# Graph network on one core: the first layer's block chain cut into two pieces, four sets of gathered rows, sums held by pairs of blocks

## The chip, the cores and the metric

The kernel runs on one core of a Trainium2 chip. A core has a matrix engine (TensorE, PE in the profile; its weight loads are listed as PEld), a vector engine (VectorE, DVE), a scalar engine (ScalarE, ACT), a general engine that here issues the gathers (GpSimd, POOL) and a queue engine that only starts transfers (SyncE, SP). Each engine works through its own list of instructions in order; semaphores tie the lists together. The tables and inputs lie in device memory (HBM), the tiles in on-chip memory (SBUF), and the results of matmuls in PSUM, which has eight banks.

The metric is the device time of one execution in microseconds, lower is better. The kernel before took 4373.74 us (median of six runs, 4352.41 to 4384.59).

## The reference, cut to what matters

Four graph layers follow each other on 6250 nodes with 128 features and about 106250 edges, sorted by their target node. Each layer is followed by a residual sum and a layer norm. The change lies in the first layer, a graph attention layer with four heads of 32 features:

```
xp = (x @ W).reshape(n, HEADS, OUT_C)
a_src = jnp.einsum('nhc,hc->nh', xp, att_src)
a_dst = jnp.einsum('nhc,hc->nh', xp, att_dst)
e = a_src[src] + a_dst[dst]                      # src, dst: the edges and one more loop per node
e = jnp.where(e >= 0, e, NEG_SLOPE * e)
m = jax.ops.segment_max(e, dst, num_segments=n)
ex = jnp.exp(e - m[dst])
denom = jax.ops.segment_sum(ex, dst, num_segments=n)
out = jax.ops.segment_sum((ex / denom[dst])[:, :, None] * xp[src], dst, num_segments=n)
return jax.nn.relu(out.reshape(n, HEADS * OUT_C) + bias)
x = _layernorm(x + the layer above)
```

So every edge fetches the row of its source node, the largest logit of each target node is found, each row is weighed with an exponential, and the rows of each target node are added up. Layers two to four (an edge-gated sum, a linear attention with a graph convolution, and a sum with two batch norms) are not touched.

## The kernel before

**Blocks.** The 6250 nodes are 50 blocks (`NB`) of 125 (`BN`). The edges of one block's targets are laid on 128 partitions (`P`) with 18 edges (`CE`) each. `quick_layer0` runs one loop over the 50 blocks (line 823); all of it is unrolled.

**One block, in the order of the source.**

1. Gather: a tile `rows` of 128 x 18 x 138 numbers, from three buffers. ACT writes its last two columns (lines 825 and 826), and POOL issues 18 indirect DMAs (line 828), each of which fetches one row of 136 numbers for each of the 128 partitions. A buffer can be filled anew only when the matmuls of the block three before have read it.
2. `dr` (lines 833 and 834, two buffers): SP loads the targets of the block's edges, the same for all of 125 partitions; DVE compares them with the partition's number (line 844); 18 small matmuls (line 848) bring each edge the terms of its target into `own_ps`, one PSUM bank.
3. `m` (line 851, two buffers): DVE compares the edges' targets with the numbers 0 to 124, which lie in PSUM as `node_ps` (a bank of its own). The result, 128 x 18 x 125, tells the summing matmuls which edge goes to which node.
4. The largest logit: ACT copies the targets and the gathered source terms (`az`) into `side`, a tile in one PSUM bank with one buffer (lines 856 and 861). DVE marks which edges of a partition have different targets (`off`, lines 857 and 859), adds (`each`, 864) and takes the maximum (`top`, 867). Twelve matmul passes (line 870, `sh_ps`) bring the maxima of neighbouring partitions, because one node's edges can reach over several.
5. The weights: DVE reduces `own_ps` to `own` (873), combines the neighbours' maxima (`near`, `carry`, `far`, `top`, 875 to 883), forms `z` (885 to 889); ACT takes the exponential into `side` (`ex`, 891) and copies it into `rows` (892); DVE multiplies the rows with it (896, "the weighing").
6. The sums: 18 matmuls in full precision (36 records in the trace; helper `gathered`, line 341) add up the rows of each node into a PSUM tile with two buffers. They wait for the weighing and are what frees the `rows` buffer and the `m` buffer.

**Work that is put off.** The functions in `left_over` are run one block later: `to_acc` copies the sums into `acc`, a tile for all 50 blocks (ACT, line 819), and after each second block `finish` (line 783) closes a pair: it adds the loop edge, divides, adds the bias and x, normalises (`norm_few`) and, through `table1`, turns the two blocks with matmuls (`t_ps`, lines 924 to 928) and stores the rows of the second layer's table. For the first 18 pairs `count` (line 1091) counts edges for later layers with 18 matmuls a pair (line 1099) and some DVE and ACT work; `sort_keys` does the groundwork in two portions (blocks 0 and 8).

**What sets the order.** No order is written out here, except on SP (`issue_after`). The framework's planner simulates the program and issues, on each engine, whatever it finds ready, earlier source first. So an instruction can stand many places ahead of its place in the source; in the trace `m` of a block is computed one block early. On the chip each engine keeps to the order planned. The framework also derives all waits: for data, for buffers to come free, and for two engines that touch one PSUM bank.

After the loop, lines 915 and 916 copy two columns of `acc` (`indeg`, `selfs`) for the second layer, whose gathers need the complete table.

Of the kernel before, what the change touches and what calls it, by code (L numbers as in the profile page):

```python
# [8 lines left out]
F32 = mybir.dt.float32  # L9
I32 = mybir.dt.int32  # L10
AF = mybir.ActivationFunctionType
ALU = mybir.AluOpType
# [11 lines left out]
N, F, BN, NB = 6250, 128, 125, 50  # L24
P, CE, NCHUNK = 128, 18, 6144
CPP = NCHUNK // P
NONE = NCHUNK - P
HEADS, OC, SLOPE = 4, 32, 0.2
# [9 lines left out]
FEW = 2  # L38
# [8 lines left out]
BF16 = mybir.dt.bfloat16  # L47
# [4 lines left out]
def kernel(ctx: ExitStack, tc: tile.TileContext, a: dict, out: bass.AP):  # L52
    nc = tc.nc
# [19 lines left out]
    indeg = const.tile([BN, NB], F32, name="indeg")  # L73
# [66 lines left out]
    def flat(t):  # L140
        return t.rearrange("p b f -> p (b f)")
# [585 lines left out]
    def quick_layer0(table):  # L727
        with tc.tile_pool(name="q0", bufs=1) as st, tc.tile_pool(name="q0w", bufs=2) as wk:
# [17 lines left out]
            acc = st.tile([BN, NB, W0], F32, name="acc")  # L746
# [36 lines left out]
            def finish(b0):  # L783
# [3 lines left out]
                nc.vector.tensor_tensor(own[:, 1], acc[:, sl, M0:M0 + HEADS], xp[:, sl, M0:M0 + HEADS], op=ALU.add)  # L787
# [12 lines left out]
                nc.vector.tensor_tensor(r, r, acc[:, sl, :F], op=ALU.add)  # L800
                rden = wk.tile([BN, FEW, HEADS], F32, name="rden")
                nc.vector.tensor_tensor(rden, acc[:, sl, A0:A0 + HEADS], part, op=ALU.add)
# [6 lines left out]
                nc.vector.scalar_tensor_tensor(flat(r), flat(r), 0.0, flat(X[:, sl, :]), op0=ALU.max, op1=ALU.add)  # L809
                norm_few(wk, b0, r, FEW)  # L810
                table1(ps, wk, w1, b0, r)

            with tc.tile_pool(name="q0_ps", bufs=2, space=PSUM) as ps:
                node_ps = ps.tile([P, BN], F32, name="node_ps", bufs=1)
                nc.scalar.copy(node_ps, node)
                left_over = []

                def to_acc(b, s):
                    nc.scalar.copy(acc[:, b, :], s)
                    if b % FEW == FEW - 1:  # L820
                        finish(b - FEW + 1)

                for b in range(NB):
                    rows = wk.tile([P, CE, W0], F32, name="rows", bufs=3)
# [6 lines left out]
                    d = dl[:, b, :]  # L831

                    dr = wk.tile([BN, P * CE], BF16, name="dr")
# [8 lines left out]
                    if b % 2 and b // 2 + 1 < NB // BPE:  # L842
                        split_terms(b // 2 + 1)
                    nc.vector.tensor_scalar(dr, dr, lane[:BN], None, op0=ALU.is_equal)
                    dr_g = dr.rearrange("d (p g) -> d g p", g=CE)
                    own_ps = ps.tile([P, CE, 6 * HEADS], F32, name="own_ps", bufs=1)
                    for g in range(CE):
                        nc.tensor.matmul(own_ps[:, g, :], dr_g[:, g, :], pieces[:, b].rearrange("p q s -> p (q s)"),  # L848
                                         start=True, stop=True)
                    m = wk.tile([P, CE, BN], F32, name="m")  # L850
                    nc.vector.tensor_tensor(m, node_ps[:, None, :].to_broadcast([P, CE, BN]),  # L851
                                            d[:, :, None].to_broadcast([P, CE, BN]), op=ALU.is_equal)

                    off = wk.tile([P, CE, CE], F32, name="off", bufs=1)
                    side = ps.tile([P, 1 + 2 * HEADS, CE], F32, name="side", bufs=1)
# [13 lines left out]
                    for k in range(2 * SPAN):  # L869
                        nc.tensor.matmul(sh_ps[:, k, :], shift[:, k, :], top[:, :, CE - 1] if k < SPAN else top[:, :, 0],  # L870
                                         start=True, stop=True)
                    own = wk.tile([P, 2 * HEADS, CE], F32, name="own")
# [19 lines left out]
                    nc.scalar.copy(rows[:, :, A0:A0 + HEADS], ex)  # L892
# [4 lines left out]
                    s = gathered(ps, m, rows, W0)  # L897
# [8 lines left out]
                    left_over.append(lambda b=b, s=s: to_acc(b, s))  # L906
# [4 lines left out]
                    if b % 2 and b // 2 < EARLY:  # L911
                        left_over.append(count(ps, wk, nth, b // 2))
                for later in left_over:
                    later()
            nc.vector.tensor_copy(indeg, acc[:, :, W0 - 2])
            nc.vector.tensor_copy(selfs, acc[:, :, W0 - 1])
# [785 lines left out]
```

## Time and profile before

| What | Value |
| --- | --- |
| Time, median of six runs | 4373.74 us (4352.41 to 4384.59) |
| The profiled execution | 4340.48 us, span 4338.7 us |
| First layer's gathers, first start to last end | 85.0 to 1411.1 us |
| First gather of the second layer | 1459.55 us |
| Busy in the span | PE 56%, DVE 50%, ACT 22%, POOL 54% |
| First layer's 900 gathers | 871.2 us busy, 968 ns each, 455.8 us of idle time before them |
| Granted TensorE clock, mean of the span | 0.707 |

The profile is one execution, recorded by the hardware. A group's line names the source line, the engine, the operation, what is written and read, how often, then the busy time and the mean duration, then the idle time of the engine just before such instructions and what ended most of it. "issue" is idle time in which the engine waited for nothing that the profile shows, "remote" means that a semaphore ended the wait and the profile does not find whose instruction set it. In a timeline a line has the start, the length, the engine, the source line, the operation, the tiles, the number of instructions merged and, in brackets, the engine's idle time before with its releaser. The starts of matmuls are recorded, their ends are modelled.

### The profile page before, as it was taken

Reading aid. Unit: us, or ns where it says so; the run is one execution under the profiler, and the core shown is the slowest. Engines: PE = TensorE matmul, PEld = TensorE weight load, DVE = VectorE, ACT = ScalarE, POOL = GpSimd, SP = SyncE. Lnnn points to the kernel's source line nnn. Section 1 sums busy time; section 2 is a strip of 40 time slices with the busy share of each in tenths; the row PEclk is TensorE's granted clock in tenths of the full one; section 3 lists DMA queues with packets and bytes.
Section 4 is the critical chain, followed back from the end, with each engine's and each line's share of the span. In section 5 each row is a group of like instructions: output and inputs, shape, how many; then the busy total and the mean of one; then the engine's idle time right before and its main releaser. Section 6 shows DMA issues by size and latency. Waiting matters only on the chain.

```text
span 4338.7 us, 46396 instructions
## 1 busy us (share of the span) xinstructions
PE 2422.0 (56%) x16000; PEld 1951.5 (45%) x16000; DVE 2179.0 (50%) x6589; ACT 948.9 (22%) x2088; POOL 2345.8 (54%) x2342
## 2 busy tenths in 40 slices
PE   2256644444444345454444444444758868978887
PEld 2245544433344234343444434344647657834444
DVE  2355555555554534454444445445747658733234
ACT  1011111111111101111111111111425435632224
POOL 4566666666666455655565555554653333066660
PEclk6566666666666566666666666666879879988888
DMA  3443233333332233333333333332323323255441
GB/s 106 93 99 74 71 74 78 79 81 75 78 76 65 73 99 94 103 97 94 94 100 91 98 97 98 93 95 75 101 84 107 106 85 116 108 194 168 158 155 56
DMA packets 187555, 422.00 MB, mean 97 GB/s; under 512 B 52792, under 2 KB 98868, under 8 KB 187300
## 3 DMA queue, kind: packets, MB, share of 16 engines
q0 software_dynamic: 88960, 214.29, 20.2%
q1 hardware_dynamic: 82026, 171.37, 11.3%
q10 hardware_dynamic: 16314, 33.19, 2.1%
q8 instruction: 129, 2.11, 0.2%
q14 instruction: 126, 1.03, 0.1%
HBM read 341.45 MB, written 77.23 MB: 96 GB/s over the span
## 4 chain that ended last, share of the span: by engine, by line
PE 30%; issue 18%; DVE 11%; another core or an unknown queue 4%; ACT 2%; POOL 1%; DMA 0%; DVEq 0%; ACTq 0%; POOLq 0%
PE acc_ps L1517 7%; PE theta L1025 7%; PE gathered L341 6%; PE acc_ps L1290 3%; DVE mw L1042 3%; DVE hit_d L1273 1%; DVE load L1220 1%; PE c_ps L1279 1%; POOL rows L1012 1%; PE s_ps L1478 1%; PE own_ps L972 1%; DVE hit_s L1270 1%; DVE to L1215 1%; DVE m L1562 1%
## 5 line engine op out<-in xcount | busy, mean ns | idle before, releaser
L1012 POOL DMA_INDIRECT rows<-table1q,e_all x900 | 879.2, 977 | 671.8 <-PE gathered L341 450.4
L828 POOL DMA_INDIRECT rows<-table0q,e_all x900 | 871.2, 968 | 455.8 <-issue 260.0
L1025 PE MATMUL theta<-parts,dr 125*128 125x128 bf16 x2700 | 355.2, 275 | 551.8 <-issue 541.5
L1025 PEld LDWEIGHTS <-dr 125*128 125x128 bf16 x2700 | 277.6, 154 | 630.4 <-issue 624.2
L1554 POOL DMA_INDIRECT rows<-table2q,e_all x252 | 291.8, 1158 | 364.0 <-PE pre_ps L1380 205.8
L341 PE MATMUL gathered<-rows,m 128*125 128x138 f32 x1800 | 342.7, 362 | 251.2 <-issue 129.9
L341 PEld LDWEIGHTS gathered<-rows,m 128*125 128x125 f32 x1800 | 321.5, 260 | 265.6 <-issue 138.8
L1554 POOL DMA_INDIRECT rows<-table3q,e_all x252 | 277.0, 1099 | 290.8 <-ACT x L1120 151.8
L1290 PE MATMUL acc_ps<-cs,x 125*128 125x250 bf16 x2700 | 397.9, 281 | 16.4 <-issue 16.0
L341 PE MATMUL gathered<-rows,mw 128*125 128x129 f32 x1800 | 302.8, 346 | 152.2 <-DVE mw L1042 138.8
L341 PEld LDWEIGHTS gathered<-rows,mw 128*125 128x125 f32 x1800 | 295.3, 258 | 157.2 <-DVE mw L1042 141.3
L1517 PE MATMUL acc_ps<-cs,x 125*128 125x500 bf16 x1350 | 325.6, 394 | 67.2 <-issue 50.9
L1290 PEld LDWEIGHTS <-x 125*128 125x128 bf16 x2700 | 272.6, 101 | 63.9 <-issue 20.9
L1280 ACT CAST cs<-c_ps 128x500 bf16<-128x500 f32 x450 | 255.4, 577 | 209.8 <-PE c_ps L1279 129.9
L851 DVE TENSOR_TENSOR m<-node_ps,dl 128x2250 f32<-128x2250 f32 x50 | 125.0, 2501 | 292.9 <-remote 260.1
L1042 DVE TENSOR_SCALAR mw<-node,dl,gw 128x125 f32<-128x125 f32 x900 | 245.7, 353 | 32.6 <-issue 28.7
L1517 PEld LDWEIGHTS <-x 125*128 125x128 bf16 x1350 | 133.0, 100 | 251.4 <-issue 116.9
L1279 PE MATMUL c_ps<-hit_d,hit_s 128*128 128x250 bf16 x900 | 186.5, 287 | 93.0 <-issue 63.0
L1029 DVE SCALAR_TENSOR_TENSOR junk<-theta,W 128x128 f32<-128x128 f32 x900 | 209.0, 284 | 15.1 <-remote 5.3
L1003 DVE TENSOR_TENSOR gram<-gram,gram_ps 128x129 f32<-128x129 f32 x25 | 7.3, 291 | 376.3 <-PE gram_ps L1002 376.3
L848 PE MATMUL own_ps<-pieces,dr 125*128 125x24 bf16 x900 | 63.1, 214 | 234.5 <-DVE own L873 143.7
L1026 DVE TENSOR_TENSOR theta<-theta,rows 128x512 f32<-128x512 f32 (+1 forms) x250 | 152.7, 638 | 62.7 <-remote 44.6
(364 smaller groups left out, 3940.0 us busy)
## 6 DMA issues: line engine op xcount, KB each, us to landing
dr<-dl_rows SPq DMA_DIRECT2D x100, 562.5 KB
counts<-cs SPq DMA_DIRECT2D x90, 625.0 KB
cs<-counts SPq DMA_DIRECT2D x45, 625.0 KB
cs<-counts ACTq DMA_DIRECT2D x45, 625.0 KB
rows<-table0q,e_all POOLq DMA_INDIRECT x900
rows<-table1q,e_all POOLq DMA_INDIRECT x900
rows<-table2q,e_all POOLq DMA_INDIRECT x252
rows<-table3q,e_all POOLq DMA_INDIRECT x252
```

The lines of the kernel that those rows point to most:

```text
L341: nc.tensor.matmul(s, m[:, g, :], rows[:, g, :], start=(g == last_first[0]), stop=(g == last_first[-1]))
L828: nc.gpsimd.indirect_dma_start(out=rows[:, g, :TW], out_offset=None, in_=table, in_offset=bass.IndirectOffsetOnAxis(ap=e_all[:, b, g:g + 1 ...
L1012: nc.gpsimd.indirect_dma_start(out=rows[:, g, :2 * F], out_offset=None, in_=table1_q, in_offset=bass.IndirectOffsetOnAxis(ap=e_all[:, b, g ...
L1025: nc.tensor.matmul(t[:, j, :], dr_g[:, g0 + j, :], y[:, k, :], start=(k == 0), stop=(k == 2))
L1026: follow(nc.vector.tensor_tensor(t[:, :n, :], t[:, :n, :], rows[:, g0:g0 + n, :F], op=ALU.subtract), b - 1)
L1029: nc.vector.scalar_tensor_tensor(junk, t[:, j, :], 0.0, w2, op0=ALU.max, op1=ALU.mult, accum_out=dot[:, g0 + j:g0 + j + 1])
L1042: last = nc.vector.tensor_scalar(mw[:, g, :], node, dl[:, b, g:g + 1], gw[:, g:g + 1], op0=ALU.is_equal, op1=ALU.mult)
L1279: nc.tensor.matmul(c_ps[:, i, :], hit_s[:, j, :, i], hit_d[:, j, :, i], start=True, stop=True)
L1280: nc.scalar.copy(cs[:, 2 * j:2 * j + 2, :], c_ps)
L1290: nc.tensor.matmul(acc_of[q], x3[:, k * SC + j, i, :], cs[:BN, j, :], start=(k == 0 and j == 0 and i == 0), stop=(k == NB // SC - 1 and j ...
L1517: nc.tensor.matmul(acc[:, :n, :], x3[:, k * SC + j, i, :], cs[:BN, :n, j, :], start=(k == 0 and j == 0 and i == 0), stop=False)
L1554: nc.gpsimd.indirect_dma_start(out=rows[:, g, :], out_offset=None, in_=table, in_offset=bass.IndirectOffsetOnAxis(ap=late_e[:, i, g:g + 1] ...
```

## The change

The loop body is cut into three functions. `gather(b)` gives out the rows buffer, the 18 gathers and the load of `dr`. `highest(b)` does the compare of `dr`, the matmuls into `own_ps`, `off`, `az`, `each`, `top` and the matmuls of the neighbours (`sh_ps`). `weigh(b)` makes `m`, reduces `own_ps`, finishes the maximum, takes the exponential, weighs the rows and adds them up. A round of the loop now reads: gather of block b, `weigh` of block b-1 with the put-off work (`step`), `highest` of block b.

What is held changes with it: `rows` has four buffers instead of three, `dr` three instead of two, `off` two instead of one, `own_ps` two banks instead of one. To pay for that bank, `node_ps` and two copies of `side` now share a single bank, in a tile named `bank`; blocks take the two copies in turn. `acc` for 50 blocks is gone; each pair has its own `acc` tile of two blocks (three buffers), and `finish` copies the pair's two columns to `indeg` and `selfs`, which replaces the two copies behind the loop. The copy of a block's sums into `acc` is ordered on ACT behind the copy of the next block's exponentials (`weighed`); this orders the list and adds no wait.

The diff, with the repeated index changes in `finish` left out:

```
-            acc = st.tile([BN, NB, W0], F32, name="acc")
...
-            def finish(b0):
+            def finish(b0, acc):
...
+                nc.vector.tensor_copy(indeg[:, sl], acc[:, :, W0 - 2])
+                nc.vector.tensor_copy(selfs[:, sl], acc[:, :, W0 - 1])
                 norm_few(wk, b0, r, FEW)
                 table1(ps, wk, w1, b0, r)
...
-                node_ps = ps.tile([P, BN], F32, name="node_ps", bufs=1)
+
+                n_side = (1 + 2 * HEADS) * CE
+                bank = ps.tile([P, 4 * P], F32, name="bank", bufs=1)
+                node_ps = bank[:, :BN]
+                side_of = [bank[:, BN + k * n_side:BN + (k + 1) * n_side].rearrange("p (h g) -> p h g", g=CE) for k in range(2)]
                 nc.scalar.copy(node_ps, node)
                 left_over = []
-
-                def to_acc(b, s):
-                    nc.scalar.copy(acc[:, b, :], s)
+                acc_of, weighed = {}, {}
+
+                def to_acc(b, s, after):
+                    if b % FEW == 0:
+                        acc_of[b // FEW] = wk.tile([BN, FEW, W0], F32, name="acc", bufs=3)
+                    copied = nc.scalar.copy(acc_of[b // FEW][:, b % FEW, :], s)
+                    if after in weighed:
+                        tc.add_manual_dep(copied.ins, weighed[after].ins.name, mybir.DependencyInfo(
+                            mybir.DependencyClass.NoSync, mybir.DependencyReason.DATA), reason="order")
                     if b % FEW == FEW - 1:
-                        finish(b - FEW + 1)
-
-                for b in range(NB):
-                    rows = wk.tile([P, CE, W0], F32, name="rows", bufs=3)
+                        finish(b - FEW + 1, acc_of.pop(b // FEW))
+
+                def gather(b):
+
+                    rows = wk.tile([P, CE, W0], F32, name="rows", bufs=4)
...
-                    d = dl[:, b, :]
-
-                    dr = wk.tile([BN, P * CE], BF16, name="dr")
+                    dr = wk.tile([BN, P * CE], BF16, name="dr", bufs=3)
...
+                    return rows, dr
+
+                def highest(b, rows, dr):
+
                     nc.vector.tensor_scalar(dr, dr, lane[:BN], None, op0=ALU.is_equal)
                     dr_g = dr.rearrange("d (p g) -> d g p", g=CE)
-                    own_ps = ps.tile([P, CE, 6 * HEADS], F32, name="own_ps", bufs=1)
+                    own_ps = ps.tile([P, CE, 6 * HEADS], F32, name="own_ps")
...
-                    m = wk.tile([P, CE, BN], F32, name="m")
-                    nc.vector.tensor_tensor(m, node_ps[:, None, :].to_broadcast([P, CE, BN]),
-                                            d[:, :, None].to_broadcast([P, CE, BN]), op=ALU.is_equal)
-
-                    off = wk.tile([P, CE, CE], F32, name="off", bufs=1)
-                    side = ps.tile([P, 1 + 2 * HEADS, CE], F32, name="side", bufs=1)
+                    d = dl[:, b, :]
+                    off = wk.tile([P, CE, CE], F32, name="off")
+                    side = side_of[b % 2]
...
+                    return b, rows, own_ps, off, top, sh_ps
+
+                def weigh(b, rows, own_ps, off, top, sh_ps):
+
+                    d = dl[:, b, :]
+                    side = side_of[b % 2]
+                    az = side[:, 1:1 + HEADS, :]
+                    m = wk.tile([P, CE, BN], F32, name="m")
+                    nc.vector.tensor_tensor(m, node_ps[:, None, :].to_broadcast([P, CE, BN]),
+                                            d[:, :, None].to_broadcast([P, CE, BN]), op=ALU.is_equal)
                     own = wk.tile([P, 2 * HEADS, CE], F32, name="own")
...
-                    nc.scalar.copy(rows[:, :, A0:A0 + HEADS], ex)
+                    weighed[b] = nc.scalar.copy(rows[:, :, A0:A0 + HEADS], ex)
...
-                    s = gathered(ps, m, rows, W0)
+                    return gathered(ps, m, rows, W0)
+
+                def step(b, s):
+
+                    nonlocal left_over
                     for later in left_over:
                         later()
...
-                    left_over.append(lambda b=b, s=s: to_acc(b, s))
+                    left_over.append(lambda: to_acc(b, s, b + 1))
...
+                behind = None
+                for b in range(NB):
+                    rows, dr = gather(b)
+                    if behind is not None:
+                        step(b - 1, weigh(*behind))
+                    behind = highest(b, rows, dr)
+                step(NB - 1, weigh(*behind))
                 for later in left_over:
                     later()
-            nc.vector.tensor_copy(indeg, acc[:, :, W0 - 2])
-            nc.vector.tensor_copy(selfs, acc[:, :, W0 - 1])
```

More of the change, by code (lines that the diff above doesn't have):

```diff
@@ L786, in finish @@
                 nc.vector.tensor_tensor(own[:, 0], xp[:, sl, A0:A0 + HEADS], xp[:, sl, M0:M0 + HEADS], op=ALU.add)
-                nc.vector.tensor_tensor(own[:, 1], acc[:, sl, M0:M0 + HEADS], xp[:, sl, M0:M0 + HEADS], op=ALU.add)
+                nc.vector.tensor_tensor(own[:, 1], acc[:, :, M0:M0 + HEADS], xp[:, sl, M0:M0 + HEADS], op=ALU.add)
                 own_f = own.rearrange("p k b h -> p (k b h)")
@@ L799, in finish @@
                                             part[:, j, :, None].to_broadcast(shape[:1] + shape[2:]), op=ALU.mult)
-                nc.vector.tensor_tensor(r, r, acc[:, sl, :F], op=ALU.add)
+                nc.vector.tensor_tensor(r, r, acc[:, :, :F], op=ALU.add)
                 rden = wk.tile([BN, FEW, HEADS], F32, name="rden")
-                nc.vector.tensor_tensor(rden, acc[:, sl, A0:A0 + HEADS], part, op=ALU.add)
+                nc.vector.tensor_tensor(rden, acc[:, :, A0:A0 + HEADS], part, op=ALU.add)
                 nc.vector.reciprocal(rden, rden)
```

## The prediction

> **What bounds the first layer now.** The gather line of the page, and that line's own view for what ended its idle time:
>
> ```profile
> span 4338.7 us, 46396 instructions
> ...
> L828 POOL DMA_INDIRECT rows<-table0q,e_all x900 | 871.2, 968 | 455.8 <-issue 260.0
> ```
>
> ```profile
> L828 POOL DMA_INDIRECT rows<-table0q,e_all x900: 941/947/1802, 85.0 to 1410.1; - x180
> ...
>   issue: 260.0, 850
>   remote: 99.9, 32
>   PE gathered L341: 90.4, 13
> ```
>
> POOL works from 85.0 to 1411.1 us. Between two gathers of one block lie 0.30 us that belong to the issue itself (850 times, 260 us); eighteen gathers cost 22.5 us. The other 195.8 us stand before a block's first gather, for a buffer. So the layer's ceiling for any better overlap is about 196 us, 4.5%. From block 19 on the blocks come every 25.6 us: 22.5 and a pause of about 3. Whom the pause waits for is seen in the timeline of two blocks:
>
> ```profile
> 1005.00 0.94 POOL L828 DMA_INDIRECT rows<-table0q,e_all  x1 [2.99 <-remote]
> ...
> 1030.26 0.28 ACT L819 COPY acc<-gathered 125x138 f32<-125x138 f32 x1 [10.06 <-remote]
> 1030.26 2.50 DVE L851 TENSOR_TENSOR m<-node_ps,dl 128x2250 f32<-128x2250 f32 x1 [6.00 <-remote]
> ...
> 1030.49 0.94 POOL L828 DMA_INDIRECT rows<-table0q,e_all  x1 [2.99 <-remote]
> ...
> 1032.75 0.16 DVE L875 TENSOR_TENSOR near<-sh_ps,gap 128x24 f32<-128x24 f32 x1
> ...
> 1037.52 1.28 ACT L891 ACT_TABLE_LOAD   x1
> 1038.81 0.29 ACT L891 ACTIVATE side<-z 128x72 f32<-128x72 f32 x1
> ...
> 1039.39 2.56 DVE L896 TENSOR_TENSOR rows<-rows,side 128x2304 f32<-128x2304 f32 x1 [3.31 <-ACT side L891]
> ...
> 1042.01 6.26 PE L341 MATMUL gathered<-rows,m 128*125 128x138 f32 x36 [4.80 <-issue]
> 1042.72 0.29 ACT L861 COPY side<-rows 128x72 f32<-128x72 f32 x1 [0.56 <-DVE off L857]
> ...
> 1055.98 2.50 DVE L851 TENSOR_TENSOR m<-node_ps,dl 128x2250 f32<-128x2250 f32 x1 [9.76 <-remote]
> ```
>
> ACT's copy of the sums, `m` and the next gather start together: three readers of one event, the end of the summing matmuls of three blocks' buffers ago. The block is one ring: weighing (to 1041.95), sums on PE (released at 1055.96), neighbours' matmuls behind them, `near` to `z` (3.4 us), exponential, weighing (2.56). From weighing to weighing that is 27.3 us (1014.7 to 1041.95) and 23.95 us (to 1065.9) in turn. Yet the releases stay 25.5 to 25.7 us apart, each about 3 us after POOL's eighteenth gather, whichever half it is. The matmuls too look quicker than they are: their 36 records begin and end within 6.3 us, the reader starts 14 us after the first. From block 18 on it is so in every block, until no gathers are left; then the reader follows at once:
>
> ```profile
> 1437.86 6.30 PE L341 MATMUL gathered<-rows,m 128*125 128x138 f32 x36 [1.09 <-DVE rows L896]
> 1444.19 0.27 ACT L819 COPY acc<-gathered 125x138 f32<-125x138 f32 x1 [7.12 <-PE gathered L341]
> ```
>
> So while POOL gathers, PE's results come 8 to 9 us late, and I can't name the resource. This weakens every saving on the ring.
>
> **The change part by part.**
>
> *The two stages.* They could overlap a block's `highest` with the `weigh` of the block before only if ACT may write the next `az` before DVE has read this block's `ex`. The trace says no: ACT's `az` copy (line 861) writes other columns of `side` than `off` (857) reads, and still starts 0.03 us after it, at 1042.72 after 1042.69; in the view of that line `off` releases it 22 times. Both copies of `side` and `node_ps` now lie in one bank, and in the source `weigh` of b-1 precedes `highest` of b. So `az` of b still follows the weighing of b-1, and I book nothing for the stages as such. If the two copies were free of each other, the 14 us of sums would cover near, exponential and weighing, and POOL's 22.5 us would be the bound: that is the lower end.
>
> The Trainium skill, "PSUM — Partial Sum Buffer", section "PSUM bank collisions raise a hardware error", has the same as a rule of the chip: two engines must not touch one bank in the same partitions together, other addresses and two readers included. By the rule the second `side` is worth nothing; by the row alone (a write behind a read) it is the same sum, and the rule only adds that `m`, a reader of that bank, must now keep clear of ACT as well.
>
> *`m` (2.50 us).* It stands in DVE's list before `near` and starts with the release, so it delays `near`: 2.3 us in one half (1056.1, when the neighbours' matmuls are through, to 1058.4), 1.05 us in the other (1031.7 to 1032.75). In the new source it needs `az` of its own block, so it comes after `top` and runs while PE still sums. Mean offer 1.7 us a block.
>
> *The pair's finish.* In every second block ACT stands before the exponential with the copies of `t_ps` and a table load: `z` is ready at 1036.1, the exponential starts at 1038.81, 2.7 us. The copy into `acc` now comes behind the next block's exponentials, so this work starts one exponential later, beside the sums; its four matmuls still wait behind them. Offer 1.35 us a block, half of it sure. What it moves: about 4.4 us of finish on DVE (lines 786 to 809 and 363 to 368, 18 instructions of 0.15 to 0.42 us) comes ahead of the next `off` (0.5 and 0.33), `each` (1.5), `top` (1.5) and `m` (2.5), with the compare of `dr` (0.84) 7.2 us. Together 11 to 12 us of DVE under 14 us of sums: hidden, but with 2 to 3 us to spare. If the sums took 7 us, as at 1437.86, 4 to 5 us would stick out.
>
> *The second `own_ps`.* DVE's reduce (line 873) waits in front of the chain, 57.2 us in 7 waits that its view calls remote (it waits for the matmuls into `own_ps` alone), most of it in the first blocks: 11.46 us at 199.75, 5.71 us at 441.92. Matmuls a block earlier into a second bank take the smaller ones. Between 0 and -57 I take -20; the longest, 16.52 us at 131.54, has POOL behind it and stays.
>
> *The fourth set.* POOL may fill one block more. In a ring that sets the pace this makes nothing quicker; POOL runs ahead once. At the end three instead of two blocks run without gathers, 14.4 to 15.8 us each (1414.0, 1429.8, 1444.2) instead of 25.6: -10. At the beginning the 21.1 us of POOL's first pause (153.2 to 174.3) fill up, but block 0's sums decide, not the gathers: 0. No transfer is added: 900 gathers, 50 loads of `dr` on SP, only earlier.
>
> *The small copies.* 50 copies in `finish` for 2 behind the loop, 0.2 us each on DVE, 10 us in all; DVE has half of its time idle and they end no chain. Without that cover, 10 us.
>
> **The sum.** `m` and finish offer up to 3.05 us a block, as much as POOL's pause (3.1). Over 49 blocks that would be -150. Against it stands that the release kept to POOL's run, not to the 27.3 or 23.95 us of its half. The ends are 0 and -150; I take a quarter, -38, because the row nearest to the question (equal releases from unequal halves) argues for little. With -20 and -10 that is -68: 4340.5 to 4272 for the profiled execution. It lies 33 us under the median of the runs, so I forecast 4305 us.
>
> **The rivals.**
>
> *POOL becomes the bound* (chance 0.13). The pauses vanish nearly all: 150 of the 195.8 us, 4224 us. For it: the ring's own work without delays is below 22.5 us. Against it: the shared bank and the late PE.
>
> *The wait comes back* (0.27). PE's results come with POOL's pause whatever the ring does; only the tail and a little of the start remain, -10 to -20: about 4360 us. For it: the equal releases. Against it: blocks 1 and 9, whose sums were read after 6.2 and 7.9 us.
>
> *Slower: four sets feed POOL without a pause, and PE is late as long as it gathers* (0.28). The place is the beginning, where three sets are filled back to back:
>
> ```profile
> 110.08 1.29 PE L848 MATMUL own_ps<-pieces,dr 125*128 125x24 bf16 x18 [17.74 <-issue]
> 131.54 0.61 DVE L873 TENSOR_REDUCE own<-own_ps 128x144 f32<-128x432 f32 x1 [16.52 <-remote]
> 133.62 2.72 PE L870 MATMUL sh_ps<-top,shift 128*128 128x4 f32 x12 [22.24 <-DVE top L867]
> 159.63 0.18 DVE L875 TENSOR_TENSOR near<-sh_ps,gap 128x24 f32<-128x24 f32 x1 [25.62 <-remote]
> ```
>
> Eighteen small matmuls were read 20 us late, twelve others 23 us late. A fourth set lengthens this by up to 22.5 us, and if each later pause has to be about 1 us longer than today's 3, 49 blocks add 49: up to +70; I price it at +50, 4424 us. It decides if the mean pause per block exceeds 3.0 us.
>
> **How the numbers follow.** The forecast's case has 0.32. About 0.5% (22 us) is what a measurement here can tell from no change. Faster: 0.32 and 0.13, 0.45. Same: 0.27. Slower: 0.28. The range leaves out the last tenth on either side: it reaches down to POOL's case, 4220, and up to the slower one, 4430. The forecast's own range is 4270 to 4345.
>
> **What would show it.** If right: the gather line's idle time falls from 455.8 by 30 to 60 us; `m` no longer starts with the copy of the sums; the exponential follows `z` within 1 us in both halves; `az` (line 861) still starts after the weighing of the block before; the three last sums stand 15 us apart after the last gather. If `az` of b starts before the weighing of b-1 ends, the bank does not tie the stages and POOL's case is near. If the first sums end later than 185 us (now 174.0) and the pauses exceed 3 us, it is the slower case. The forecast fails if the planner puts `finish` between `top` and the neighbours' matmuls, or leaves `m` before `near`.

## The result, and the profile after

The changed kernel took 4396.57 us (median of 28 runs, 4375.12 to 4435.23) against 4373.32 us for the kernel before (65 runs): a ratio of 1.0059, 95% interval 1.0041 to 1.0076. It is 0.6% slower; the forecast said 1.6% faster. The page's lines that answer to those of before:

```profile
span 4378.7 us, 46483 instructions
...
L840 POOL DMA_INDIRECT rows<-table0q,e_all x900 | 874.5, 972 | 479.3 <-issue 257.9
```

The gathers' idle time did not fall by 30 to 60 us, it rose from 455.8 to 479.3 us. The timeline of two steady blocks (start, duration, engine, line, operation; in brackets the idle time and what ended it):

```profile
743.95 0.94 POOL L840 DMA_INDIRECT rows<-table0q,e_all  x1 [3.63 <-remote]
744.76 0.18 DVE L896 TENSOR_TENSOR near<-sh_ps,gap 128x24 f32<-128x24 f32 x1 [5.70 <-PE sh_ps L881]
...
748.42 2.56 DVE L917 TENSOR_TENSOR rows<-rows,bank 128x2304 f32<-128x2304 f32 x1 [0.63 <-ACT rows L913]
...
751.03 7.43 PE L341 MATMUL gathered<-rows,m 128*125 128x138 f32 x36 [2.09 <-DVE rows L917]
751.75 0.29 ACT L872 COPY bank<-rows 128x72 f32<-128x72 f32 x1 [0.56 <-DVE off L868]
...
759.89 0.82 DVE L858 TENSOR_SCALAR dr<-dr,lane 125x2304 bf16<-125x2304 bf16 x1 [8.10 <-DMA dr<-dl_rows]
...
763.50 1.50 DVE L878 TENSOR_REDUCE top<-each 128x72 f32<-128x1296 f32 x1
...
765.24 2.49 DVE L891 TENSOR_TENSOR m<-bank,dl 128x2250 f32<-128x2250 f32 x1
...
769.52 0.22 ACT L837 COPY rows<-ones 128x18 f32<-128x18 f32 x1 [17.34 <-remote]
769.76 0.95 POOL L840 DMA_INDIRECT rows<-table0q,e_all  x1 [3.20 <-remote]
770.15 0.18 DVE L896 TENSOR_TENSOR near<-sh_ps,gap 128x24 f32<-128x24 f32 x1 [2.09 <-PE sh_ps L881]
```

Four things are to be seen. `az` (line 872, 751.75) still follows the weighing of the block before (ends 750.98). The sums of 751.03 are over in the records at 758.46, but the set they free is used at 769.52 only, about 3 us after the last gather of the run (it ends at 766.56): the wait came back as it was, one block later in the chain. `top` of the odd block stands at 763.50, nearly 12 us behind its `az`: DVE's list has the compare of a later block's `dr` ahead of it, and DVE waited 8.10 us for that load (759.89). And `m` is through at 767.73, 2.4 us ahead of `near`: it holds `near` up no longer, as the prediction wanted, and the next gather still starts 3.20 us after the last.

In this document a pause is the time from the end of a block's last gather to the start of the next block's first, and a slot is the time from one block's first gather to the next block's first. For a second pair of profiles both kernels ran once more on one chip (the chips are told of below); they give the layer as a balance. Times in us:

| | before, first profile | before, second | changed, first | changed, second |
| --- | --- | --- | --- | --- |
| execution | 4340.5 | 4365.3 | 4380.5 | 4391.3 |
| first gather starts | 85.0 | 84.8 | 85.1 | 85.7 |
| pauses, blocks 1 to 4 | 37 | 38 | 11 | 12 |
| pauses, blocks 5 to 19 | 64 | 79 | 107 | 103 |
| pauses, blocks 20 to 49 | 94 | 98 | 100 | 98 |
| the 50 runs of 18 gathers | 1130.6 | 1127.2 | 1134.0 | 1135.3 |
| last gather's end to the last sums' copy | 33.1 | 32.2 | 48.1 | 48.3 |
| last sums' copy starts | 1444.2 | 1459.6 | 1486.1 | 1481.9 |

The second pair has 22.3 us between its last copies, of 26.0 us in all, and the balance closes: +0.9 at the start, -26, +24 and 0 in the pauses, +8.1 in the gathers themselves, +16.1 behind the last one, 23 from rounded rows. Of the 42 us between the two first profiles the rest can be put down to the executions: that of before was one of the shortest of its kernel, and its pauses in blocks 5 to 19 alone are 15 us below those of its second profile. So the first blocks did save 26 us, and more than that was given back in three places.

*Behind the last gather.* The copies of the last four sums, first profile of the changed kernel (its last gather ends at 1438.0):

```profile
1446.02 0.27 ACT L827 COPY acc<-gathered 125x138 f32<-125x138 f32 x1
...
1461.11 0.28 ACT L827 COPY acc<-gathered 125x138 f32<-125x138 f32 x1
...
1476.37 0.27 ACT L827 COPY acc<-gathered 125x138 f32<-125x138 f32 x1
...
1486.14 0.27 ACT L827 COPY acc<-gathered 125x138 f32<-125x138 f32 x1 [6.22 <-PE gathered L341]
```

Three blocks come after it, 15 us each and the last 10, where the kernel before had two. POOL's lead of a block is a block more to be worked off when POOL is done.

*Blocks 5 to 19*, where PE also counts keys for the later layers (`c_ps`). The timeline of block 7's exponential and the gathers of block 11, that wait for its sums:

```profile
379.56 0.47 PE L955 MATMUL t_ps<-ident,X 125*128 125x125 f32 x1 [2.49 <-ACT X L370]
379.86 0.21 DVE L910 TENSOR_TENSOR z<-z 128x72 f32<-128x72 f32 x1
...
386.08 0.94 POOL L840 DMA_INDIRECT rows<-table0q,e_all  x1 [0.30 <-issue]
389.55 0.27 ACT L957 COPY t<-t_ps 128x125 f32<-128x125 f32 x1 [9.65 <-remote]
...
391.13 0.30 ACT L912 ACTIVATE bank<-z 128x72 f32<-128x72 f32 x1
...
401.63 0.94 POOL L840 DMA_INDIRECT rows<-table0q,e_all  x1 [14.61 <-PE gathered L341]
```

`z` is ready at 380.07 (379.86 and 0.21). ACT has the pair's finish ahead of the exponential, and in it the copy of a transposition that PE did at 379.56 and that ACT sees at 389.55, 2.5 us after POOL's run. The exponential is 11 us late, and POOL pauses 14.6 us. Over blocks 1 to 18 the exponential followed `z` by 16 and 19 us in all before (the two profiles), by 56 and 40 us now.

*The gathers themselves*: 8.1 us; see the first experiment.

### The profile page after: what moved, and what is told of

The parts are those of the page before. It is cut to its first block, busy times and chain, and to the rows that moved or that the text cites. A ratio compares the mean times of both kernels' runs of the same rounds, so it can differ in the third digit from the quotient of the medians.

```text
span 4378.7 us, 46483 instructions
## 1 busy us (share of the span) xinstructions
PE 2436.0 (56%) x16000; PEld 1972.9 (45%) x16000; DVE 2185.4 (50%) x6637; ACT 941.3 (21%) x2088; POOL 2350.7 (54%) x2342
## 4 chain that ended last, share of the span: by engine, by line
PE 30%; issue 18%; DVE 10%; another core or an unknown queue 4%; ACT 2%; POOL 1%; DMA 0%; ACTq 0%; DVEq 0%; POOLq 0%
PE theta L1056 7%; PE acc_ps L1548 7%; PE gathered L341 7%; PE acc_ps L1321 3%; DVE mw L1073 3%; DVE hit_d L1304 1%; PE c_ps L1310 1%; DVE load L1251 1%; POOL rows L1043 1%; PE s_ps L1509 1%; PE own_ps L1003 1%; DVE hit_s L1301 1%; DVE to L1246 1%; DVE m L1593 1%
## 5 line engine op out<-in xcount | busy, mean ns | idle before, releaser
L1043 POOL DMA_INDIRECT rows<-table1q,e_all x900 | 878.9, 977 | 672.6 <-PE gathered L341 451.8
L840 POOL DMA_INDIRECT rows<-table0q,e_all x900 | 874.5, 972 | 479.3 <-issue 257.9
L881 PE MATMUL sh_ps<-top,shift 128*128 128x4 f32 x600 | 120.6, 309 | 286.2 <-issue 179.0
L881 PEld LDWEIGHTS sh_ps<-top,shift 128*128 128x128 f32 x600 | 121.7, 286 | 290.6 <-issue 287.0
```

Source lines behind the costliest of these rows:

```text
L840: nc.gpsimd.indirect_dma_start(out=rows[:, g, :TW], out_offset=None, in_=table, in_offset=bass.IndirectOffsetOnAxis(ap=e_all[:, b, g:g + 1 ...
L1043: nc.gpsimd.indirect_dma_start(out=rows[:, g, :2 * F], out_offset=None, in_=table1_q, in_offset=bass.IndirectOffsetOnAxis(ap=e_all[:, b, g ...
```

## The experiments

The runs fell on chips of two kinds, and no number can be read without that. On four (that of the second pair above among them) and on that of the first measurement the kernel before takes 4365 to 4470 us; on two others 3487 us. Each comparison below is with the kernel before on the same chip. "Pauses" are given for blocks 1 to 4, 5 to 19 and 20 to 49.

**Both kernels on another chip.** Unedited.

> The changed kernel again, unedited, so that it stands beside the runs before it, which took 3487 us for the kernel before and not 4373. Theory C (how late PE's results are released while POOL gathers belongs to the chip that a run is on; where they are not late POOL gathers without a pause, slot 22.5 to 23.1 us, and only what follows the last gather can differ): 3490 to 3500 us where the kernel before takes 3487, and 4390 to 4400 us where it takes 4373. Theory D (the same lateness on every chip, and the difference is in the kernels run so far): a slot of 25.8 us again in either case.

> The kernel before, unedited, for its profile beside the changed kernel's on the same chip. Theory C: where the time is near 3487 us, POOL's pause between two blocks' gathers is 0.3 us as between any two gathers, the slot is 22.5 to 23.1 us, and the difference to the changed kernel is made behind the last gather; where the time is near 4373 us, the pause is some 3 us and the slot 25.6. Theory D: the pause is 3 us in either case.

3495.65 us against 3487.69: 1.0029 (1.0016 to 1.0041). The gather lines of before and of the changed kernel there:

```profile
L828 POOL DMA_INDIRECT rows<-table0q,e_all x900 | 872.9, 970 | 274.8 <-issue 265.4
```

```profile
L840 POOL DMA_INDIRECT rows<-table0q,e_all x900 | 878.9, 977 | 274.8 <-issue 267.5
```

Theory C held. POOL's idle time is the 0.30 us of issue and hardly anything else, the slot is 22.8 to 22.9 us, and PE's results are read within a microsecond (in the kernel before: neighbours' matmuls from 558.10 to 559.57 us, `near` at 560.28, in the midst of a run of gathers). What I expected of the difference is wrong: behind the last gather both take 23 us. The difference is in the gathers, 872.9 and 878.9 us, and the last one starts 6.0 us later. Gathers that lie over a DVE instruction take longer: over the compare of `dr` (2304 numbers, bf16) there were 38 of over 1.05 us, 11.6 us more than the usual 0.945, before 37 with 10.8; over the counting's compare 5.9 us and 3.5; over `each` 2.8 and 0.4; over the finish's last sum (line 808) 2.0 and none; over `m` 1.1 and none.

**One part undone**, first on a chip with 3487 us.

```
-                behind = highest(b, rows, dr)        (and weigh of the block before ahead of it)
+                step(b, weigh(*highest(b, rows, dr)))
```

> Undoes the two stages alone: every block is gathered, its highest terms taken and its messages weighed in one go, as before; the four sets, the sums by pairs and the small copies stay. Theory A (a block's slot in the steady part is set by when PE's results are released, some 3 us after POOL's run of gathers, and not by the length of the chain): steady slot within 0.2 us of the changed kernel's 25.84, time within 15 us of its 4396. Theory B (the two stages cost the time, because the pair's finish and m now stand ahead of top): the steady slot returns to 25.6 or less, the counting blocks lose no lead, and the time falls by 30 us or more, to 4360 or lower.

```
-                    rows = wk.tile([P, CE, W0], F32, name="rows", bufs=4)
+                    rows = wk.tile([P, CE, W0], F32, name="rows", bufs=3)
```

> Undoes the fourth set alone: three sets of gathered rows, everything else as changed. Theory A: the steady slot stays within 0.3 us of 25.84, and the wait behind the last gather falls from 47.8 us to some 33, because two blocks and not three are left: 10 to 20 us faster than the changed kernel unless the start loses more than that. Theory B' (the two-stage chain needs the fourth set, since it holds each set a block longer): the slot grows to 28 us or more, over 100 us slower than the changed kernel.

One stage 1.0015 (1.0004 to 1.0027), three sets 1.0022 (1.0011 to 1.0034). The numbers for theories A and B were set for 4396 us and apply only in their differences: nothing here is limited by chain or sets. So both again on a chip where before takes 4371 us:

> The two stages undone alone, as in the run of that name, on another chip. Where the kernel before takes some 3487 us: 1.0015 of it again, within 0.15%. Where it takes 4373 to 4452: the changed kernel is at 1.0059 there, and the pairs alone at 1.001. Theory G (the two stages are what costs): 1.001 to 1.003. Theory H (the fourth set is what costs, by a third block left behind the last gather): 1.004 to 1.008.

> The fourth set undone alone, as in the run of that name, on another chip. Where the kernel before takes some 3487 us: 1.002 of it again. Where it takes 4373 to 4452: theory H (the fourth set costs, by a third block left behind the last gather): 1.001 to 1.003. Theory G (the stages cost): 1.004 to 1.008. Theory B' (the two stages hold each set a block longer, so that three are too few): 1.015 or more.

and, where before takes 4452 us, both undone at once (`bufs=3` and the one-stage loop; the sums by pairs stay):

> One stage and three sets: of the change there stays the sums by pairs, the ordered sums' copies, the second own_ps and the small copies. Theory A: without the fourth set the wait behind the last gather is that of the kernel before, and nothing else moves the slot: within 0.2% of the kernel before on whichever chip. Theory E (the finish by pairs with its ordered copies is what costs, by DVE work that falls beside POOL's gathers and ahead of the next top): 0.2% or more slower than the kernel before, as the changed kernel is, although both the stages and the set are undone.

| | ratio (95%) | pauses | behind the last gather | slot, blocks 20 to 43 |
| --- | --- | --- | --- | --- |
| changed | 1.0059 (1.0041 to 1.0076) | 12, 103, 98 | 48.3 | 25.85 |
| one stage | 1.0033 (0.9991 to 1.0076) | 11, 103, 100 | 48.4 | 25.82 |
| three sets | 1.0049 (1.0014 to 1.0084) | 31, 109, 100 | 31.2 | 25.80 |
| pairs alone | 1.0010 (0.9983 to 1.0037) | 36, 101, 104 | 31.4 | 26.01 |
| before | 1 | 38, 79, 98 | 32.2 | 25.68 |

The pauses of the changed kernel and of before are those of the second pair; the ratio of the changed kernel is that of the first measurement. The ratios overlap too much to rank the parts (G against H is not settled by them); the profiles, one execution each, go further. Both kernels with four sets have 11 to 12 us of pauses in the first blocks and 48 us at the end, all with three have 31 to 38 and 31 to 33. So the fourth set is worth about -20 to -26 and +16. The stages move no pause. Blocks 5 to 19 have 101 to 109 us in all four kernels of the table with the new sums. And the slot, 25.7 to 26.0, shows no effect of stages, sets or sums beyond what the chips differ by.

**Does PE's work or POOL's run set the release?** One own_ps matmul in place of 18 (this kernel leaves out the edges' own terms for 17 of 18 groups), then each of them twice:

```
-                    for g in range(CE):
-                        nc.tensor.matmul(own_ps[:, g, :], dr_g[:, g, :], ...)
+                    nc.tensor.matmul(own_ps, dr_g[:, 0, :], ... .to_broadcast([BN, CE, 6 * HEADS]), ...)
```

```
+                    for g in list(range(CE)) * 2:
```

> The changed kernel with one own_ps matmul a block in place of 18 (the first group's match is used for all groups, so the edges' own terms are left out for the rest). PE has 34 instructions less per block (17 matmuls, 17 weight loads), and the chain of the block is not shortened, because own_ps is ready long before it is read. Theory A1 (while POOL gathers, every PE instruction lengthens the slot by some 0.05 us, the slope that separates the stages of the trace): slot 25.84 - 1.8 = 24.0 us, time lower by 60 to 90 us. Theory A2 (the release waits for POOL's run alone, however few instructions PE has): slot 25.6 to 25.9, time within 12 us.

> The changed kernel with every own_ps matmul made twice (the same result): 36 PE instructions more per block, 1.2 us of PE's own time. Theory A1 (0.05 us of slot per PE instruction while POOL gathers): slot 25.84 + 1.9 = 27.7 us, time higher by 70 to 100 us. Theory A2 (the release waits for POOL's run alone): slot 25.8 to 26.0, time within 12 us.

On a chip with 3487 us: 1.0034 (1.0022 to 1.0045) and 1.0025 (1.0015 to 1.0035), no effect beside the changed kernel's 1.0029. Again where before takes 4380 us:

> As the run with one own_ps matmul a block (the edges' own terms are left out for 17 of 18 groups), on another chip. Where the kernel before takes some 3487 us, POOL has no pause that could shrink and the time stays within 0.2% of the changed kernel's. Where it takes 4370 to 4450 (slot 25.8, pause 3.3): theory A1 (PE falls behind while POOL gathers, by an amount that goes with the number of its instructions): slot 23.5 to 24.5, time 60 to 100 us below the changed kernel's 1.006. Theory A2 (the release comes a fixed 3 us after POOL's run, whatever PE has to do): slot 25.6 to 25.9, time within 0.4% of it.

> As the run with every own_ps matmul made twice, on another chip. Where the kernel before takes some 3487 us: within 0.2% of the changed kernel. Where it takes 4370 to 4450: theory A1: slot 27.3 to 28.3, time 60 to 110 us above the changed kernel's 1.006. Theory A2: slot 25.8 to 26.1, time within 0.4% of it.

> The kernel before, unedited, for its profile beside the changed kernel's on one chip: the profile of before that the prediction read was of an execution of 4340 us, 33 us under the median of its kernel, that of the changed kernel one of 4380, 16 us under its own. Where the time is 4370 to 4450: the slot is 25.6 to 25.9 and the last copy of the sums ends at 1445 to 1475 us, so that part of the 42 us between the two first profiles was the execution and not the change.

> The changed kernel, unedited, for its profile beside the one of the kernel before on the same chip. Where the time is 4390 to 4470: slot 25.8 to 26.1, the wait behind the last gather 45 to 50 us where the kernel before has 31 to 34, and the lead at block 4 (some 20 us) gone by block 20.

Once: 0.9960 (0.9918 to 1.0001), about 1% under the changed kernel and between what the two theories set, pauses 10, 75, 93, slot 25.71. Twice: 1.0173 (1.0095 to 1.0251), pauses 26, 130, 120, slot 26.46. The last two are the second pair of profiles above. Neither theory has it all. With 34 PE instructions less the steady slot falls by 0.14 us and not by 1.8: there the release keeps to POOL's run (A2). In the counting blocks, where PE has most to do, the same edit takes 28 us off the pauses, and twice the matmuls put 28 on and lengthen the steady slot too (A1). So there is a floor of about 3 us, and above it PE's backlog. In the run with one matmul the floor is seen bare: the twelve neighbours' matmuls are through at 962.89 in the records, `near` reads them at 969.43, 3 us after POOL's last gather (966.44).

**The stages freed of each other.** Each side gets a bank of its own. First with `node` read from SBUF and one `own_ps` (where before takes 4452 us):

```
+                side_of = [ps.tile([P, 1 + 2 * HEADS, CE], F32, name=f"side{k}", bufs=1) for k in range(2)]
+                node_ps = node[:, :BN]
```

> The changed kernel with its two sides in two PSUM banks of their own (node is read from SBUF by m, and own_ps has one buffer in place of two, which gives the banks). Step 1 of the prediction (the two stages can't overlap because the sides and node_ps lie in one bank): az of a block now starts as soon as its rows are there and ACT is free, ahead of the messages of the block before in most blocks, where it follows them in 50 of 50 of the changed kernel. What that is worth, theory A (the slot is set by POOL's run and by when PE's results are released): within 12 us of the changed kernel on the same chip. Theory B (the chain's length sets the slot): 40 us or more faster where the slot is 25.8 us.

1.0056 (1.0019 to 1.0093). `az` now starts ahead of the end of the earlier weighing in 36 of 49 blocks (in the changed kernel in none). Pauses 8, 58, 92, but the runs of gathers grew to 1231 us; in the timeline:

```profile
697.08 2.50 DVE L889 TENSOR_TENSOR m<-node,dl 128x2250 f32<-128x2250 f32 x1 [21.12 <-remote]
697.31 3.09 POOL L838 DMA_INDIRECT rows<-table0q,e_all  x1 [4.36 <-PE own_ps L860]
```

A gather beside `m` takes 2.75 us on average instead of 0.945, in 50 of 50 blocks: 90 us. `m` had the same form and duration before, but one operand in PSUM. Then `m` with `node` from SBUF and the targets from the side in PSUM:

> As the run with two banks, but m takes dl's copy from the side in PSUM and node from SBUF, so that one of its two operands is in PSUM again. In the run with two banks the stages did overlap, but 50 of 50 m stood beside a gather that took 1.8 us longer (90 us in all). Theory F (a wide DVE operation with both operands in SBUF holds POOL up, and that hid the gain of the overlap): the 90 us go, POOL's gathers sum to 875 to 885 us again, and the time is that of the two banks less 60 to 100 us: 4360 to 4410 where the kernel before takes 4452, 3485 to 3500 where it takes 3487. Theory A (the overlap is worth nothing, because the release of the set waits for POOL's run): the pauses come back to 3 us a block and the time is within 0.4% of the changed kernel's.

The 90 us are gone (runs 1126 us), and the time is 1.037 (1.0323 to 1.0417): pauses 11, 115, 225. Last, `node_ps` in a third bank, for which `own_ps` and `sh_ps` share one:

> The changed kernel with each side in a PSUM bank of its own and node_ps in a third, for which own_ps and sh_ps share one bank with one buffer: the stages can overlap, and m keeps one operand in PSUM and waits for no side. Theory F (in the first run with two banks the overlap was worth something, and POOL lost it beside m): POOL's run is 22.5 us again and not 24.8, the pause goes below 2 us, slot 24.5 or less, 50 us or more below the changed kernel where that takes 1.006 of the kernel before. Theory A2 (the release comes 3 us after POOL's run whatever the chain does): slot 25.5 to 26.0, within 0.5% of the changed kernel. Theory I (the shared bank and its single buffer put more waits for PE in a row, as in the second run with two banks, 1.037): 1.015 or more. Where the kernel before takes 3487 us: within 0.3% of it in every case, as POOL has no pause there.

1.0573 (1.0505 to 1.0642), runs 1126 us, pauses 8, 119, 306, in pairs of 0.3 and 20 us. The timeline of one pair; POOL gathers without a pause from 1003.6 to 1048.5:

```profile
1016.48 1.29 PE L863 MATMUL own_ps<-pieces,dr 125*128 125x24 bf16 x18 [4.67 <-remote]
...
1045.85 0.35 PE L1130 MATMUL c_ps<-of,above 128*128 128x100 bf16 x1 [2.45 <-issue]
...
1047.55 0.95 POOL L839 DMA_INDIRECT rows<-table0q,e_all  x1 [0.30 <-issue]
...
1053.55 0.35 PE L1130 MATMUL c_ps<-of,above 128*128 128x100 bf16 x1 [0.35 <-issue]
1054.40 0.61 DVE L894 TENSOR_REDUCE own<-own_ps 128x144 f32<-128x432 f32 x1 [31.81 <-PE c_ps L1130]
```

Matmuls of 1016.48 are read 38 us later, after both runs; while POOL gathers, PE issues a counting matmul only every 2.1 to 2.8 us and waits for nothing that the profile shows; soon after it the steps are 1.4 and then 0.7 us. The reduce of `own_ps` stands ahead of the weighing in DVE's list, so everything behind it waits too. Theory F's first half held (POOL's loss beside `m`), its second fell in both runs. All three pay for the banks with the second buffer of `own_ps`, and the last puts `sh_ps` into its bank besides, so what the overlap alone is worth they do not show. That the first of the three had the shortest pauses is open too: its POOL stood still 1.8 us once in every run of gathers, and whether that lets PE's results through was not tried.

**The order.** `m` behind `top` (an order added; before takes 4365 us), and the copy of the sums without its order (before takes 4469 us):

```
+                    tc.add_manual_dep(made.ins, topped[b].ins.name, ...)       # made: m, topped[b]: the reduce into top
```

> The changed kernel with m ordered behind top, which it stood ahead of in every second block, so that the neighbours' matmuls start 2.5 us earlier there. Theory B (the order in the chain costs): 20 us or more below the changed kernel, 1.001 or less where that is at 1.006. Theory A2 (the release waits for POOL's run, so 2.5 us in the chain are worth nothing): within 0.25% of the changed kernel; POOL's run per block may fall by up to 0.05 us, as m no longer stands beside the same gathers.

```
-                    if after in weighed:
-                        tc.add_manual_dep(copied.ins, weighed[after].ins.name, ...)
```

> The changed kernel without the order that puts the copy of a block's sums behind the next block's exponentials; four sets, two stages, the sums by pairs and all else stay. Numbers are for a chip where the kernel before takes 4370 to 4450 us. Theory J (the ordered copy, with the pair's finish behind it, is what lengthens POOL's pauses in the counting blocks 5 to 19 from 64 to 79 us before to 99 to 109 in every kernel with the new sums): pauses of blocks 5 to 19 fall to 60 to 85 us, the exponential's delays behind z over blocks 1 to 18 from some 40 us to 20, and the time by 15 to 30 us, to 0.999 to 1.003 of the kernel before. Theory K (it is m and the second stage's place in DVE's list): the pauses of blocks 5 to 19 stay at 95 to 110 us and the time within 0.2% of the changed kernel's 1.006. In both the pauses of blocks 20 to 49 stay at 95 to 105 us, and the wait behind the last gather at 45 to 50.

`m` behind `top`: 1.0038 (0.9984 to 1.0092), pauses 10, 99, 99, slot 25.81, last copy at 1476.4 against 1481.9. By the profiles the order of `m` is worth some 5 us and not 20; the interval alone could not exclude either. The wait for `dr` went with it: from `az` to `top` it is 56 us in all over blocks 20 to 43, near the 50 of the kernel before, where the changed kernel has 174 to 189, and the pauses stay. So neither `m` nor the late `top` is what holds POOL up in the steady blocks. The same odd block as in the timeline of the changed kernel:

```profile
742.06 0.29 ACT L872 COPY bank<-rows 128x72 f32<-128x72 f32 x1 [0.56 <-issue]
...
745.34 1.45 DVE L878 TENSOR_REDUCE top<-each 128x72 f32<-128x1296 f32 x1
...
747.03 2.49 DVE L891 TENSOR_TENSOR m<-bank,dl 128x2250 f32<-128x2250 f32 x1
...
760.88 0.94 POOL L840 DMA_INDIRECT rows<-table0q,e_all  x1 [3.48 <-remote]
```

`top` follows its `az` by 3.3 us here and by 12 us there, and the next gather starts 3.48 us after the last all the same.

Without the order: 1.0051 (1.0021 to 1.0081), pauses 11, 76, 158. Theory J held where it looked: the counting blocks return to what before had in the second pair, 76 us where the six profiles with the order in which PE's work and the shared bank are as changed have 99 to 109 (on several chips), and the exponential's delays to 17 us. It missed its time and the steady blocks, where the pauses are 60 us longer than in the changed kernel's second profile: unordered, the copy can stand in ACT's list ahead of the next `az` and exponential and wait there for late sums. How much of the 60 us is the order's is open. That profile is of another chip, of which there is none of the kernel before, and its last sums' copy starts at 1524.4, 42.5 us later than in that profile, while the ratios, 1.0051 and 1.0059, are alike, so part of it should belong to the chip or to the execution. What the order for blocks from 20 on alone would be worth was not run; the counting blocks' rows make it some 27 us at most.

## Why the prediction was wrong

*The two stages (booked at nothing).* Right that they don't overlap: `az` follows the earlier weighing in every block. That overlap, if free, would make POOL the bound is not borne out: with banks of their own the stages did overlap, and in the two runs in which nothing held POOL up the time rose by 3.7% and 5.7%. The lower end of the range rested on that. It is not refuted either, since those runs gave up the second buffer of `own_ps` for it.

*`m` and the finish (a quarter of 3.05 us a block, -38).* This is the step that failed, and close to the way the prediction named: the planner left `m` ahead of `top` in 25 of 50 blocks, and in the others put the compare of a later `dr` ahead of `top`, whose load DVE waits for, and some 1.7 us of the finish (`az` to `top` over blocks 20 to 43: 50 us before, 174 to 189 now, of which the wait for `dr` makes 81 to 96). But that is not what it cost, for with `m` behind `top` this is gone and the pauses stay. In blocks 20 to 49 the saving is zero (98.5 us of pauses before, 98.1 now) because the release keeps to POOL's run; I had seen the equal releases from unequal halves and should have taken the row at its word. (By the rows shown there PE's sums were read 7.7 us after their recorded end, not 8 to 9; nothing in the sum hangs on it.) In blocks 5 to 19 the sign was wrong: I put the finish one exponential later "beside the sums" and named its four matmuls as waiting behind those, but not that ACT waits for each of them in turn, in front of the next exponential, with PE late. It is +24 us in the second pair (+44 in the first), and it goes when the order goes. PE's backlog has a part in it: with one `own_ps` matmul these pauses are 75 us too, although the order stands and the exponential's delays are still 44 us.

*The second `own_ps` (-20).* The waits did fall, from 71.8 to 33.4 us by the view of that reduce, and the long one at the start stayed. No pause shows it as a gain: the pairs alone, which have the second bank, have 36, 101 and 104 us where before has 38, 79 and 98.

*The fourth set (-10).* Both terms were wrong. The start, booked at 0, gave -26: the 21 us of POOL's first pause and part of the next did not come again within four blocks. The tail, booked at -10, was +16: I counted three blocks at 15 us against 25.6 in the ring, but by then the ring's time runs under POOL's gathers, and what counts is the work left when these end, a block more. That -26 and +16 make the -10 that was booked is luck: two errors cancel.

*The small copies (0).* The cover I named was DVE's idle time. What I left out is that DVE beside POOL costs POOL: 3.4, 8.1 and 6.0 us in the changed kernel's gathers, in the three pairs of profiles, from several DVE operations that moved; I can't say how much of it belongs to the 50 copies.

*The rivals.* "The wait comes back" describes blocks 20 to 49 of the second pair to a tenth of a microsecond per block, but its 4360 us had the tail at -10. "Slower, with four sets back to back" has the right sign and was placed wrongly: at the start, the neighbours' matmuls are read at 162.88 where before it was 159.63, no 22 us later. The whole comes to 4396.6, inside the range, on the side that was given 0.28. Of the 90 us between the booked -68 and the 22 us of the second pair, 62 lie in `m` and the finish, 20 in the second `own_ps`, the rest in the gathers and at the start.

## What to carry to other kernels

Before a buffer is added ahead of a ring that sets the pace, book its tail: the lead is paid back as one more block of work after the producer's end, and only what the lead saves at the start is there to pay it. An engine's in-order list turns one late result into a delay for all that stands behind its reader, so move a reader of late results only after asking what is queued behind it, in each stage of the layer apart: here one order cost some 27 us in the counting blocks and saved up to 60 us, part of which may be the chip's, in the steady ones. When releases stay equally spaced under unequal work, price savings on the ring at nothing until the lock itself has been moved.

## What the runs showed of the hardware

PE's lateness while POOL gathers belongs to some chips and not to others: on two the same program has POOL at work without a pause (22.8 us a block, 3487 us), on the others the mean pause of blocks 20 to 49 is 3.1 to 3.5 us in both kernels and in every edit that left the banks, the order of the sums' copy and PE's work as they were (4365 to 4470 us). It is not the whole of what sets the chips apart: of the 878 us between the profiles of the kernel before on the two kinds, 225 lie ahead of the last sums' copy of the first layer, the rest behind it. The granted clock hardly explains it: from 200 to 1200 us it is 0.62 on the one kind, 0.64 and 0.65 on the other. Nor do fetches of instructions by DMA: 129 packets of 16 KB, about 1 us each, in both. The resource stays unnamed.

A DVE operation on two SBUF operands (`m`, 128 x 2250 in fp32, 2.50 us) held back a gather that POOL issued beside it by 1.8 us, 50 times of 50; with one operand in PSUM the same operation did so in 7 and 8 blocks of the changed kernel's runs, by 0.15 us. The Trainium skill, "SBUF — State Buffer", section "Who interferes with whom", has the contention of such an operation with a POOL instruction that reads SBUF, and infers that the making of a transfer's descriptors is not touched by a `tensor_tensor`. The measurement agrees with the first if a gather, which takes its row numbers from `e_all` in SBUF, counts as such an instruction: it is held back. Whether at the reading of the row numbers or at the descriptors no run here shows.
